# A sparse four-layer graph network on one core: half of a table's copies on VectorE, late variances on ScalarE, sends held back, ring slots freed by whole blocks

## The chip, the cores and the metric

The kernel runs on one NeuronCore of a Trainium2 chip. The core has five engines with instruction queues of their own: TensorE (PE), VectorE (DVE), ScalarE (ACT), GpSimd (POOL) and SyncE (SP). The metric is the device time of one execution in microseconds.

## The reference

A graph of 4096 nodes with 256 features passes through four layers of graph attention. The adjacency matrix `adj` is 4096 x 4096 int32, symmetric, with ones on its diagonal and few others. Every layer normalizes, applies a relu, lets each node attend to its neighbours, and adds the result to `x`:

```python
def _layernorm(x, axis=-1, eps=1e-5):
    m = jnp.mean(x, axis=axis, keepdims=True)
    v = jnp.var(x, axis=axis, keepdims=True)
    return (x - m) / jnp.sqrt(v + eps)

# layer 0: four heads, leaky_relu 0.2, softmax over neighbours, elu
Wh = (h @ W).reshape(n, heads, d)
e = leaky_relu(s_i[:, None, :] + s_j[None, :, :], 0.2)   # s_i, s_j: Wh . a
e = where((adj == 0)[:, :, None], -inf, e)
out = elu(einsum('ijh,jhd->ihd', softmax(e, axis=1), Wh))
# layer 1: one head, slope 0.01, returns h + att @ node, with h = node @ W
# layer 2: four heads, slope 0.2, weights, biases and phis
# layer 3: q, k, v with biases, scores q.k / 8, mask from adj, att @ v
for layer in layers:
    x = x + layer(maximum(_layernorm(x), 0))
```

## The kernel before

The class `Sparse` computes with lists of neighbours and not with the dense matrix. Nodes stand in 32 blocks of 128, sorted by their number of neighbours; `CAPS` gives the largest number in each block, from 23 down to 3. A block's rows lie on the 128 partitions.

**Scan (`scan`, L254).** SP loads `adj` in 128 pieces of 512 KB, ACT turns each into fp8 and sums it (L277, six raw buffers), PE multiplies it by marks (L519, L529), and DVE takes the eight largest of each stretch (L531); from these ACT writes the numbers of the neighbours (L566, L569). Beside that, `tick(k)` (L371) makes the first table: `table(u)` takes a pair of blocks through relu (L342), transposes (L349), ACT's copy from PSUM (L352), two products (L986) and the copies of the products from PSUM to SBUF (L356); SP writes four blocks at a time to the table in DRAM. The scales of a group of four blocks come from `stats` (DVE's sums and ACT's logarithm), `roots` and `scaled`, which `tick` issues at every second pair. `cast(upto)` keeps ACT's casts going between the pairs. Then POOL fetches the first six neighbours of each node (L993, tile `s_g`), one indirect DMA for one neighbour of 128 nodes, and PE sums them.

**Late (`late`, L1056).** The remaining neighbours of the first layer, 19 groups of one or two blocks in the order `LATE`, 93 gathers. `fill(i)` (L1097) first sends out finished rows by `deliver()` (L1086, one indirect DMA of a block's rows of the second table, L1010), then fetches up to four groups ahead into the ring `s_ring`. `settle(i)` (L1195) adds the sums, takes the elu, calls `norms_of` (L636: DVE's BATCH_NORM_STATS2 at L642 and BATCH_NORM_AGGREGATE at L643, ACT's logarithm, exponential and square, three small operations of DVE), then relu, transposes, ACT's copy (L1224), the product with the next weights and the copy of the rows to send (L1233). A block is put on the list `pending` when its rows are made. POOL's order is given by hand: a send comes behind the fetch before it, and the next fetch behind the send.

**Layers 1 to 3 (`layer(l)`, L1263).** For each of the 32 blocks in `ORDER`, `fill` (L1273) fetches the neighbours' rows of the block four places ahead into the ring (`AHEAD`; 18432 floats a partition, which makes 69, 64, 69 and 36 slots in layers 0 to 3), 270 gathers a layer. Then come `scores` (L1359), `weigh` and `settle`. `weigh` multiplies the block's slots by their shares on DVE (L1466, eight slots at once) and lets PE add them up in PSUM (tile `s_acc`): x (L1450), the node's own row `s_me` (L1458), then two slots at a time (L1471). `settle` adds the two halves of the sum on DVE (L1491, or L1487 in layer 3); `normed` and `turned` make the next h, its transposes (L974) and ACT's copy (L976), and `advance` makes the next table's rows. The table's rows go to DRAM on SP, and layer 3's results by POOL (L1010, `out_dram`). The first gather of layer 1 waits for every send of late; the first of layers 2 and 3 wait for the whole table.

The blocks run interleaved: block i is scored and weighed while block i−1 is settled and block i−2 goes through the product. A gather into a slot waits for the product that last read the slot; PE's products each signal for that. All engines run in program order here, so whatever stands behind a waiting instruction on its engine waits too.

## Time and profile before

| | |
|---|---|
| median of four runs | 2037.8 us (2027.78 to 2039.83) |
| profiled execution | 2025.78 us, span 2024.1 us |
| granted TensorE clock, mean | 0.754 |
| busy: PE, DVE, ACT, POOL | 1132.6, 1111.6, 534.9, 1141.2 us |
| POOL's indirect DMAs, gathers into `s_ring` and `s_g` | 900 and 192 |
| sends to the second table | 32 |
| HBM read, written | 273.00 MB, 35.00 MB |

A line of the groups reads: source line, engine, operation, output tile <- input tiles, shapes, number of instructions | busy time, mean time of one in ns | idle time of the engine just before them, and what ended most of it. In a timeline, the start and the duration stand in front of an instruction and the idle time before it and its releaser behind. A line of waits gives the total, the number and the longest wait. Lines are those of the kernel before.

### The profile page before, as it was taken

How to read it: one execution, taken by the hardware profiler on the slowest of the kernel's cores; microseconds unless marked ns; L12 is line 12 of the kernel's file. 1: busy time of each engine (PE TensorE's matmuls, PEld its weight loads, DVE VectorE, ACT ScalarE, POOL GpSimd, SP SyncE). 2: the span in 40 equal slices, each digit the busy share in tenths (PEclk: the TensorE clock that was granted, in tenths of full speed). 3: DMA queues.
4: the chain of work that ended last, by engine and by line, in shares of the span. 5: the costliest groups of instructions: out<-in, count | busy, mean ns of one | idle time of the engine just before them, and what ended most of it. 6: DMA issues, size and time to landing. Idle time of an engine off the chain costs nothing. (4 is left out here: it accounts for less than half of the span.)

```text
span 2024.1 us, 14506 instructions
## 1 busy us (share of the span) xinstructions
PE 1132.6 (56%) x3035; PEld 582.5 (29%) x3035; DVE 1111.6 (55%) x2651; ACT 534.9 (26%) x1754; POOL 1141.2 (56%) x1241
## 2 busy tenths in 40 slices
PE   6678777415673354566773146556669334545545
PEld 4323322113341122333441023223335112222222
DVE  5476777533682233344552125555558466777857
ACT  6854552011252022233341012222335000000000
POOL 1455656776545756666614756565530656766664
PEclk9877777756796676787886667788889566767768
DMA  7999885574422433444412434333321656666663
GB/s 256 339 348 313 305 301 179 183 193 126 131 74 79 118 98 102 110 113 116 115 38 78 109 88 111 97 107 96 99 75 37 197 168 177 202 179 191 176 180 104
DMA packets 125913, 309.12 MB, mean 153 GB/s; under 512 B 35029, under 2 KB 53464, under 8 KB 125817
## 3 DMA queue, kind: packets, MB, share of 16 engines
q0 software_dynamic: 66832, 203.64, 35.5%
q1 hardware_dynamic: 58984, 104.46, 14.7%
q8 instruction: 28, 0.46, 0.1%
q14 instruction: 69, 0.56, 0.1%
HBM read 273.00 MB, written 35.00 MB: 152 GB/s over the span
## 5 line engine op out<-in xcount | busy, mean ns | idle before, releaser
L993 POOL DMA_INDIRECT s_ring<-s_tab,s_near x900 | 853.5, 948 | 581.0 <-issue 255.4
L1471 PE MATMUL s_acc<-s_ring,s_ident 128*128 128x512 f32 (+1 forms) x858 | 422.2, 643 | 32.1 <-issue 19.1
L993 POOL DMA_INDIRECT s_g<-s_tab,s_keep x192 | 183.4, 955 | 178.6 <-DMA s_raw<-in_adj_dram 67.4
L1471 PEld LDWEIGHTS s_acc<-s_ring,s_ident 128*128 128x128 f32 x858 | 183.4, 218 | 249.5 <-issue 213.4
L1466 DVE TENSOR_TENSOR s_ring<-s_ring,s_shares 128x2048 f32<-128x2048 f32 (+1 forms) x153 | 233.0, 1554 | 0.0
L986 PE MATMUL s_ps<-s_we_l,s_ht 128*128 128x264 f32 x256 | 95.3, 518 | 176.7 <-issue 75.8
L1491 DVE TENSOR_REDUCE s_rx<-s_acc 128x256 f32<-128x512 f32 x64 | 44.1, 689 | 253.9 <-remote 180.4
L986 PE MATMUL s_ps_kv<-s_wkv,s_ht 128*128 128x512 f32 x128 | 87.9, 823 | 156.7 <-issue 95.5
L1458 PE MATMUL s_acc<-s_me,s_ident 128*128 128x256 f32 x192 | 74.2, 474 | 174.3 <-DVE s_me L1454 95.8
L519 PE MATMUL s_pt<-s_low,s_mark_True 128*128 128x512 fp8e4 x256 | 97.0, 464 | 72.2 <-ACT s_keep L569 23.7
L277 ACT ACTIVATE s_low<-s_raw 128x1024 fp8e4<-128x1024 int32 x128 | 133.8, 1046 | 12.0 <-DMA s_raw<-in_adj_dram 7.2
L976 ACT COPY s_ht<-s_pht 128x256 f32<-128x256 f32 x64 | 23.8, 372 | 361.5 <-remote 232.1
L986 PEld LDWEIGHTS s_ps<-s_we_l,s_ht 128*128 128x128 f32 x256 | 58.1, 245 | 204.2 <-ACT s_ht L976 80.8
L1418 ACT ACTIVATE s_shares<-s_e 128x40 f32<-128x40 f32 (+7 forms) x64 | 12.6, 197 | 334.1 <-DVE s_e L1415 142.9
L531 DVE MAX8 s_cand<-s_pt 128x8 f32<-128x256 f32 x256 | 93.3, 418 | 13.8 <-PE s_pt L529 13.8
L629 PE MATMUL s_ae<-s_g,s_ident 128*128 128x512 f32 x192 | 95.8, 629 | 2.5 <-DVE s_g L620 2.1
L1458 PEld LDWEIGHTS s_acc<-s_me,s_ident 128*128 128x128 f32 x192 | 41.1, 229 | 191.6 <-DVE s_me L1454 100.1
L1394 DVE TENSOR_TENSOR s_ring<-s_ring,s_shares 128x2048 f32<-128x2048 f32 (+7 forms) x47 | 78.5, 1671 | 17.8 <-DMA s_ring<-s_tab,s_near 17.7
L986 PEld LDWEIGHTS s_ps_kv<-s_wkv,s_ht 128*128 128x128 f32 x128 | 28.5, 247 | 187.5 <-issue 121.7
L1397 DVE TENSOR_REDUCE s_e<-s_ring 128x32 f32<-128x2048 f32 (+7 forms) x47 | 78.9, 1679 | 1.6
L1487 DVE TENSOR_REDUCE s_out<-s_acc 128x256 f32<-128x512 f32 x32 | 22.0, 687 | 90.6 <-remote 67.3
L1010 POOL DMA_INDIRECT s_tab<-s_rx,s_near x32 | 32.8, 1025 | 66.4 <-ACT s_rx L1233 44.9
(284 smaller groups left out, 1797.9 us busy)
## 6 DMA issues: line engine op xcount, KB each, us to landing
s_raw<-in_adj_dram SPq DMA_DIRECT2D x128, 512.0 KB
s_ring<-s_tab,s_near POOLq DMA_INDIRECT x900
s_rx<-s_placed SPq DMA_DIRECT2D x32, 262.0 KB
s_tab<-s_kv SPq DMA_DIRECT2D x32, 256.0 KB
s_tab<-s_rx SPq DMA_DIRECT2D x32, 132.0 KB
s_keep<-in_x_dram SPq DMA_DIRECT2D x8, 512.0 KB
s_vself<-s_tab SPq DMA_DIRECT2D x32, 128.0 KB
s_tab<-s_keep SPq DMA_DIRECT2D x7, 528.0 KB
```

What stands on the lines that cost most here:

```text
L277: nc.scalar.activation(low[r][:, quarter(q)], raw.pop(q), AF.Copy, saturate=False, accum_out=self.sums[:, r, h : h + 1],)
L519: nc.tensor.matmul(pt, lhsT=self.mark[k], rhs=lo[:, k * PAIR + g * IB : k * PAIR + (g + 1) * IB], start=(k == 0), stop=False,)
L531: nc.vector.max(out=cand[:, g * (IB // CH) + k, :], in_=pt[:, ts(k, CH)])
L629: nc.tensor.matmul(acc, lhsT=self.ident, rhs=g[:, :, k, 0:D], start=False, stop=(k == E - 1))
L986: self.nc.tensor.matmul(ps[:, :width], lhsT=ht[:, c, :], rhs=w[:, c, :], start=(c == 0 and bias is None), stop=(c == KC - 1),)
L993: return self.nc.gpsimd.indirect_dma_start(out=out, out_offset=None, in_=table[:, :], in_offset=bass.IndirectOffsetOnAxis(ap=idx, axis=0),)
L1394: nc.vector.tensor_tensor(kq, kq, q.unsqueeze(1).to_broadcast([P, m, D]), ALU.mult)
L1397: nc.vector.tensor_reduce(e[:, k0 : k0 + m, :], kq.rearrange("p k (h d) -> p k h d", h=4), AX.X, ALU.add)
L1458: nc.tensor.matmul(acc[:, 0, :], lhsT=self.ident, rhs=mev, start=False, stop=False)
L1466: nc.vector.tensor_tensor(v, v, p[:, k0 : k0 + m, :].unsqueeze(3).to_broadcast([P, m, H, D // H]), ALU.mult)
L1471: nc.tensor.matmul(acc[:, 0:n, :], lhsT=self.ident, rhs=g[:, k : k + n, v0 : v0 + D], start=False, stop=(k + 2 >= G),)
L1491: nc.vector.tensor_reduce(xt, acc.rearrange("p u d -> p d u"), AX.X, ALU.add)
```

## The change

- In the first table, one of the two copies of a pair (L356) is made by DVE instead of ACT. `tick` issues `roots` and `scaled` at odd places, behind the pairs, and `stats` at even ones; `constants()` is called at place 5 instead of 4, and the casts run one place later (`cast(k - 5)`).
- In late, `settle` takes the sums of x and of its squared deviations by accumulating operands (DVE's sum per block, ACT's square per block) instead of the statistics of `norms_of`.
- `deliver(8)` in late's `fill` holds back the last eight blocks; what is left goes at the end. `known()` is called at group 3 instead of 1. In layer 3 up to three finished blocks are held before one is sent.
- In layers 1 to 3 the node's own row is added last (it was second), the first slot has a product of its own, and then come pairs. The first gather of a block waits for the last product of every old block that its slots overlap (`past`); the other gathers wait for no product. Some dependencies are declared as covered by others (`declare_no_dep`).

```diff
--- before.py
+++ after.py
@@ -352,8 +352,8 @@
             nc.scalar.copy(ht, pt.rearrange("p (k c r) -> p k c r", k=2, c=KC))
             ps = [self.times(ht[:, k], self.we0, W, f"t0_{2 * u + k}") for k in range(2)]
             yield
-            for k in range(2):
-                nc.scalar.copy(self.keep[:, 2 * u + k, D : D + W], ps[k])
+            for k, copy in ((0, nc.scalar.copy), (1, nc.vector.tensor_copy)):
+                copy(self.keep[:, 2 * u + k, D : D + W], ps[k])
             g = u // 2
             m = 2 if g == groups - 1 else 4
             if u % 2 or m == 2:
@@ -376,11 +376,11 @@
                 if u in made:
                     next(made[u])
             g = k // 2 + 1
-            if k % 2 == 0 and g < groups:
+            if k % 2 and g < groups:
                 roots(g)
-                if g + 1 < groups:
-                    stats(g + 1)
                 scaled(g)
+            if k % 2 == 0 and g + 1 < groups:
+                stats(g + 1)
 
         whole = []
         for j in range(nt // 2):
@@ -415,10 +415,10 @@
 
         for k in range(2 * groups + 2):
             tick(k)
-            if k == 4:
+            if k == 5:
                 self.constants()
             if k >= 6:
-                cast(k - 4)
+                cast(k - 5)
             if k - 8 in range(8):
                 mark(k - 8)
         for at in range(8, end + 1):
@@ -1039,6 +1039,7 @@
             self.norms = big.tile([P, 2, nt], F32, name="s_norms")
             self.both = big.tile([P, 2], F32, name="s_both")
             self.has = big.tile([P, nt, CAPS[0]], F32, name="s_has")
+            self.past, self.took_x, self.seen = [], {}, []
             E = mybir.EngineType
             with tc.manual_schedule(engines={E.PE, E.DVE, E.Activation, E.SP}):
                 self.reload()
@@ -1083,8 +1084,8 @@
             self.fetched = f
             return f
 
-        def deliver():
-            while pending:
+        def deliver(held_back=0):
+            while len(pending) > held_back:
                 b = pending.pop(0)
                 s = self.send(self.tab[1], self.own(b), self.listed[b]).ins
                 if self.fetched is not None:
@@ -1096,7 +1097,7 @@
 
         def fill(i):
             nonlocal at
-            deliver()
+            deliver(8)
             while todo and todo[0] <= i + 4:
                 m, K = size(todo[0])
                 s = (at if at + m * K <= slots else 0) if K else 0
@@ -1202,18 +1203,34 @@
             nc.scalar.activation(ex, ex, AF.Copy, bias=-1.0)
             yield
             nc.vector.scalar_tensor_tensor(ex, ex, 0.0, xt, ALU.min, ALU.add)
-            nc.vector.scalar_tensor_tensor(xt, acc, 0.0, ex, ALU.max, ALU.add)
-            norm = self.norms_of(pool, xt if m > 1 else xt[:, 0, :], m, f"0_{i}", self.minus)
-            for _ in range(m if m > 1 else 0):
-                next(norm)
-            next(norm)
+            y = pool.tile([P, 8, 2], F32, name=f"s_y_0_{i}", tag="y0", bufs=3)
+            sum_, minus, q, log, root, less, r, at = (y[:, k, 0:m] for k in range(8))
+            for u in range(m):
+                nc.vector.scalar_tensor_tensor(
+                    xt[:, u, :], acc[:, u, :], 0.0, ex[:, u, :], ALU.max, ALU.add,
+                    accum_out=sum_[:, u : u + 1],
+                )
+            act = nc.scalar.activation
+            act(minus, sum_, AF.Copy, scale=-1.0 / D)
+            junk = pool.tile([P, D], F32, name=f"s_junk_{i}", tag="junk", bufs=1)
+            for u in range(m):
+                act(
+                    junk, xt[:, u, :], AF.Square, bias=minus[:, u : u + 1],
+                    accum_out=q[:, u : u + 1],
+                )
+            act(log, q, AF.Ln, bias=self.eps, scale=1.0 / D)
+            act(less, q, AF.Identity, bias=self.minus, scale=-0.5 / D)
+            act(root, log, AF.Exp, scale=-0.5)
+            act(log, root, AF.Square)
             yield
-            rn = next(norm)
+            nc.vector.tensor_tensor(less, log, less, ALU.mult)
+            nc.vector.scalar_tensor_tensor(r, less, 1.5, root, ALU.add, ALU.mult)
+            nc.vector.tensor_tensor(at, minus, r, ALU.mult)
             h = part(i, D, 2 * D)
             for u in range(m):
                 nc.scalar.activation(
                     h[:, u, :], xt[:, u, :], AF.Relu,
-                    bias=rn[:, m + u : m + u + 1], scale=rn[:, u : u + 1],
+                    bias=at[:, u : u + 1], scale=r[:, u : u + 1],
                 )
             pt = self.pp.tile([P, IB], F32, tag="ps", name=f"s_pht_0_{i}")
             for u in range(m):
@@ -1244,7 +1261,7 @@
 
         for i in range(len(LATE) + 3):
             fill(i)
-            if i == 1:
+            if i == 3:
                 self.known()
             if i == 5:
                 self.share_place()
@@ -1269,6 +1286,7 @@
         ring = self.ring[:, : slots * wide].rearrange("p (k w) -> p k w", w=wide)
         todo, held, at = list(ORDER), {}, 0
         made = []
+        past = self.past
 
         def fill(i):
             nonlocal at
@@ -1287,9 +1305,27 @@
                 if l == 3:
                     vs[j] = self.pool.tile([P, D], F32, name=f"s_vself_{j}", tag="vself", bufs=5)
                     nc.sync.dma_start(out=vs[j], in_=self.tab[3][ts(j, P), D:])
+                ends = [
+                    e for a, b, e in past if a < (s + room) * wide and s * wide < b
+                ]
+                past[:] = [
+                    (a, b, e) for a, b, e in past if not (a < (s + room) * wide and s * wide < b)
+                ]
                 for k in range(K):
                     at_k = self.near[:, j, k : k + 1]
                     g = self.fetch(ring[:, s + k, :], self.tab[l], at_k).ins
+                    if k == 0:
+                        for _, last in ends:
+                            self.tc.add_manual_dep(
+                                g, last.name,
+                                mybir.DependencyInfo(
+                                    mybir.DependencyClass.Sync, mybir.DependencyReason.DATA
+                                ),
+                                reason="the block's slots are free",
+                            )
+                    for some, _ in ends:
+                        for m in some:
+                            self.tc.declare_no_dep(g, m, reason="its block's last is waited for")
                     for told in self.told:
                         self.tc.add_manual_dep(
                             g, told.name,
@@ -1328,7 +1364,7 @@
         def third(d):
             if d in rows:
                 next(rows.pop(d), None)
-            while made and (len(made) > 1 or todo == []):
+            while made and (len(made) > 3 or todo == []):
                 self.send(*made.pop(0))
 
         S, N = 1, 2
@@ -1343,7 +1379,8 @@
             third(e)
             product(d)
             sums[b] = self.weigh(l, b, vs.pop(b) if l == 3 else self.rows[b][:, 0:D], g, p)
-            del held[b]
+            start, end = held.pop(b)
+            past.append((start * wide, end * wide, self.read))
             settle(c)
         z, y, x, w = ORDER[-1:-5:-1]
 
@@ -1371,7 +1408,7 @@
                 nc.scalar.activation(e[:, :G, 0], g[:, :G, D], AF.Identity, bias=src)
                 nc.scalar.activation(e[:, K, :], mine[:, D : D + H], AF.Identity, bias=src)
             else:
-                nc.vector.tensor_tensor(e[:, K, :], mine[:, D : D + H], src, ALU.add)
+                first = nc.vector.tensor_tensor(e[:, K, :], mine[:, D : D + H], src, ALU.add)
                 nc.vector.tensor_tensor(
                     e[:, :G, :], g[:, :G, D : D + H],
                     src.unsqueeze(1).to_broadcast([P, G, H]), ALU.add,
@@ -1383,7 +1420,9 @@
             if more:
                 self.more_scores(l, mine, g[:, KEPT, :], e)
             slope = 0.01 if l == 1 else 0.2
-            nc.vector.scalar_tensor_tensor(ek, ek, slope, ek, ALU.mult, ALU.max)
+            steep = nc.vector.scalar_tensor_tensor(ek, ek, slope, ek, ALU.mult, ALU.max)
+            if l == 2:
+                self.tc.declare_no_dep(steep.ins, first.ins, reason="another sum comes after it")
         else:
             q = self.shares[:, IB - D :]
             nc.scalar.copy(q, mine[:, 0:D])
@@ -1426,7 +1465,9 @@
         nc.vector.tensor_scalar(
             eq[:, :K, :], g[:, :K, W : WL - 1], self.own_f[:, b : b + 1], None, ALU.is_equal
         )
-        nc.vector.tensor_reduce(self.has[:, b, :K], eq[:, :K, :], AX.X, ALU.max)
+        self.seen.append(
+            nc.vector.tensor_reduce(self.has[:, b, :K], eq[:, :K, :], AX.X, ALU.max).ins
+        )
 
     def weigh(self, l, b, me, g, made):
 
@@ -1447,18 +1488,22 @@
         self.turns += 1
         v0 = 0 if l < 3 else D
         acc = self.pacc.tile([P, 2, D], F32, tag="acc", name=f"s_acc_{l}_{b}")
-        nc.tensor.matmul(
+        self.took_x[b] = nc.tensor.matmul(
             acc[:, 1, :], lhsT=self.ident, rhs=self.x[b], start=True, stop=False
         )
+        some = []
         mev = pool.tile([P, D], F32, name=f"s_me_{l}_{b}", tag="me", bufs=3)
-        nc.vector.tensor_tensor(
+        own = nc.vector.tensor_tensor(
             mev.rearrange("p (h d) -> p h d", h=H), me.rearrange("p (h d) -> p h d", h=H),
             p[:, K, :].unsqueeze(2).to_broadcast([P, H, D // H]), ALU.mult,
         )
-        nc.tensor.matmul(acc[:, 0, :], lhsT=self.ident, rhs=mev, start=False, stop=False)
         if more:
             rows = self.more_rows(l, p, g[:, KEPT, :])
-            nc.tensor.matmul(acc[:, 0, :], lhsT=self.to_row, rhs=rows, start=False, stop=False)
+            some.append(
+                nc.tensor.matmul(
+                    acc[:, 0, :], lhsT=self.to_row, rhs=rows, start=False, stop=False
+                ).ins
+            )
         step = 2 if b in ORDER[-2:] else AT_ONCE
         for k0 in range(0, G, step):
             m = min(step, G - k0)
@@ -1466,12 +1511,21 @@
             nc.vector.tensor_tensor(
                 v, v, p[:, k0 : k0 + m, :].unsqueeze(3).to_broadcast([P, m, H, D // H]), ALU.mult
             )
-            for k in range(k0, k0 + m, 2):
-                n = min(2, G - k)
-                nc.tensor.matmul(
-                    acc[:, 0:n, :], lhsT=self.ident, rhs=g[:, k : k + n, v0 : v0 + D],
-                    start=False, stop=(k + 2 >= G),
-                )
+            k = k0
+            while k < k0 + m:
+                n = min(2, k0 + m - k) if some else 1
+                some.append(
+                    nc.tensor.matmul(
+                        acc[:, 0:n, :], lhsT=self.ident, rhs=g[:, k : k + n, v0 : v0 + D],
+                        start=False, stop=False,
+                    ).ins
+                )
+                k += n
+        last = nc.tensor.matmul(
+            acc[:, 0, :], lhsT=self.ident, rhs=mev, start=False, stop=True
+        ).ins
+        self.tc.declare_no_dep(last, own.ins, reason="the slots' products come after it")
+        self.read = (some, last)
         return acc
 
     def settle(self, l, b, acc, made):
@@ -1488,7 +1542,10 @@
             made.append((self.out, self.own(b), y))
             yield None
             return
-        nc.vector.tensor_reduce(xt, acc.rearrange("p u d -> p d u"), AX.X, ALU.add)
+        s = nc.vector.tensor_reduce(xt, acc.rearrange("p u d -> p d u"), AX.X, ALU.add)
+        self.tc.declare_no_dep(
+            s.ins, self.took_x.pop(b).ins, reason="the sum's last product comes after it"
+        )
         yield from self.normed(pool, xt, f"{l + 1}_{b}")
 
     def advance(self, l, b, ht, made):
@@ -1530,9 +1587,11 @@
     def symmetric(self):
 
         nc, ok = self.nc, self.ok[:, 4:5]
-        nc.vector.scalar_tensor_tensor(
+        all_of = nc.vector.scalar_tensor_tensor(
             self.has, self.away[:, :, : CAPS[0]], 1.0 / FAR, self.has, ALU.mult, ALU.max
         )
+        for i in self.seen[:-1]:
+            self.tc.declare_no_dep(all_of.ins, i, reason="the last of them is waited for")
         nc.vector.tensor_reduce(self.both[:, 0:1], self.has, AX.XY, ALU.min)
         nc.vector.tensor_reduce(ok, self.both, AX.X, ALU.min)
         nc.vector.tensor_scalar(ok, ok, 0.5, None, ALU.is_ge)
```

## Prediction

> **What bounds the kernel now.** I read the page's groups first, then the waits of POOL, then the timeline at one place, then windows. No engine is busy for more than 57% of the span (PE 1132.6 us, DVE 1111.6, POOL 1141.2 of 2024.1), so the end is set by turns between engines. Groups of the page (busy time, mean ns, idle time before them, what ended it):
>
> ```profile
> L993 POOL DMA_INDIRECT s_ring<-s_tab,s_near x900 | 853.5, 948 | 581.0 <-issue 255.4
> L1491 DVE TENSOR_REDUCE s_rx<-s_acc 128x256 f32<-128x512 f32 x64 | 44.1, 689 | 253.9 <-remote 180.4
> L976 ACT COPY s_ht<-s_pht 128x256 f32<-128x256 f32 x64 | 23.8, 372 | 361.5 <-remote 232.1
> L1487 DVE TENSOR_REDUCE s_out<-s_acc 128x256 f32<-128x512 f32 x32 | 22.0, 687 | 90.6 <-remote 67.3
> ```
>
> A gather costs POOL 0.95 us and 0.30 us to the next ("issue", 255.4 us over about 800 of them), so 1.25 us. The three readers of PE's results in PSUM wait 254 + 362 + 91 us for something that the profile calls "remote". The timeline shows what it is:
>
> ```profile
> 663.02 8.96 PE L1471 MATMUL s_acc<-s_ring,s_ident 128*128 128x512 f32 x16 [0.98 <-issue]
> 701.82 0.69 DVE L1491 TENSOR_REDUCE s_rx<-s_acc 128x256 f32<-128x512 f32 x1 [33.45 <-issue]
> 705.79 0.69 PE L974 MATMUL s_pht<-s_ident,s_h 128*128 128x128 f32 x2 [31.23 <-issue]
> 727.78 0.95 POOL L993 DMA_INDIRECT s_ring<-s_tab,s_near  x1 [0.30 <-issue]
> 729.83 0.37 ACT L976 COPY s_ht<-s_pht 128x256 f32<-128x256 f32 x1 [22.79 <-remote]
> 741.20 0.94 POOL L993 DMA_INDIRECT s_ring<-s_tab,s_near  x1 [12.47 <-ACT s_rx L1507]
> ```
>
> PE's sums of block 0 are recorded done at 671.98, and DVE starts to add them at 701.82. PE's two transposes are done at 706.48, ACT copies them at 729.83: 1.1 us after POOL's last gather of an unbroken row ended (728.73). Meanwhile nearly everything but POOL stands still; columns of the windows: length, then busy (instructions) of PE, PEld, DVE, ACT, POOL, clock, DMA share, GB/s:
>
> ```profile
> 670.00:700.00 30.00, 4.56 (x14) 2.28 (x12) 0.00 (x0) 0.00 (x0) 22.68 (x24) 0.63 0.44 118
> 1498.50:1574.00 75.50, 66.20 (x198) 36.48 (x198) 58.21 (x144) 35.95 (x140) 0.04 (x1) 0.96 0.11 40
> ```
>
> The first stretch has 24 gathers and nothing on DVE and ACT. The second is layer 2's tail without gathers: there the same work goes at full pace. My reading: while POOL issues gathers without a break, PE's completions reach the other engines late, and they come through when POOL pauses. A layer thus alternates between a gathering POOL and computing engines, instead of doing both. That it depends on how many completions PE signals is my assumption; no row shows it alone. POOL's own waits (total, times, longest) say what the pauses are:
>
> ```profile
> POOL s_ring L993 <- PE s_acc L1471: 85.8, 37, 9.1
> POOL s_ring L993 <- DMA s_vself<-s_tab: 75.8, 1, 75.8
> POOL s_ring L993 <- DMA s_tab<-s_rx: 56.6, 1, 56.6
> POOL s_tab L1010 <- ACT s_rx L1233: 44.9, 10, 10.1
> ```
>
> Stages by POOL's first DMA: late 413.2, layer 1 632.8, layer 2 1080.2, layer 3 1574.4, last send ends 2020.6.
>
> **The change, part by part.** The sum is made on the profiled execution, 2025.8 us (span 2024.1 and 1.7 around it); the median of the four runs is 2037.8, 0.6% above, and I scale at the end.
>
> **First table.** 16 of 32 copies of L356 (0.38 us each) leave ACT, 6.1 us, from an engine that is busy 9.94 of 10 us in 40–50; DVE, busy 4.77 there, takes them. Turning the roots behind the pairs, and the cast by one place, moves work in the same queues and with each cast the issue of a raw load on SP: ACT's casts (1.05 us each) come one tick later, which could cost up to three of them, 3.1 us. Then DMA at 300–350 GB/s sets the scan. Between −6.1 and +3.1; I take −3, the ACT time less one such cast.
>
> **Late variances.** DVE loses 32 x (0.414 + 0.182) = 19.1 us of statistics (L642, L643) and gains 13 further starts where a two-block sum of L1205 is cut in two, some 0.2 us each: net −17. ACT gains 32 squares with an accumulator (0.42 + 0.19) and 19 small operations of 0.23: +24, on 69.3 us in a stage of 219.6. DVE is the busier there (52.1 of 60 us in 550–610), ACT has 30 us free in the same window. Between −17 and +7 (ACT's gain less DVE's loss, if the chain of a group runs through both); nearest to −12.
>
> **Sends held back.** POOL waits 44.9 us for L1233 and 15.3 for L1224 ahead of sends: these go for the first 66 gathers, which now run in one row from 413 to 496 (66 x 1.25). Behind the waiting sends stood the gathers. But the pause at 470.5–481.6 is also what let PE's completions through, in a burst at 478.5; now they wait for about 497. The work behind it moves by up to 20 us. The 60 us that POOL no longer waits can't be had whole: the last groups are bound by DVE, and 22 sends now stand at the end (x 1.3 = 29 us). So between −31 and +20; nearest is the row of the burst, +20, of which I take off the 15 us for L1224: +5. known() at i == 3 moves a few DVE operations behind the first groups: nothing, hidden by DVE's wait for the first gathers there.
>
> **Blockwise freeing.** Removed: the signal of most products. In the built programs PE signals 1184 times before and 651 after on the sparse path; in layers 1 and 2 about 9.5 times a block becomes 4 (last product, transposes, scores' two tables), in layer 3 6.5 becomes 1. POOL's separate waits on PE fall from 440 to 121; a satisfied one cost nothing in the trace (gap of 0.30 us with and without). Added: one matmul of 256 columns (0.43 us) in blocks of an even number of slots, on a PE that idles half of the layer: nothing, covered by DVE's next product of 1.55 us. Also added: the first gather of a block waits for the last product of every old block that it overlaps. Behind this gather stand all later gathers on POOL, and behind these, the scores of four blocks on. In layer 2 POOL already stalls 22 times for L1471 (67.0 us); each would end later by the rest of a block, at most four products x 0.86 = 3.4 us. By the ring's layout (64, 69 and 36 slots) a gathered block overlaps two old ones 5, 5 and 4 times. Over 5 (layer 2's borders) to 22 stalls that is +17 to +75, if POOL were the bound throughout.
> Layer bounds: POOL alone needs 270 x 1.25 = 337.5 us a layer. Layer 1 gathers in 390.8 us (53 over) and then waits 56.6; layer 2 in 418.1 (81 over) and waits 75.8; layer 3 takes 446, with 32 sends x 1.3 = 42 and a tail of 28 in it, so 39 over.
> With half the completions I take that a quarter to a third of the excess goes: layer 1, 53 x 0.28 = −15 (ends −53 − 7 of tail, and +5); layer 2, 81 x 0.25 = −20 (ends −81, and +75 by the stalls above); layer 3, with one completion of PE in six left and 91 us of DVE waiting for just these, 28 of the 39 (ends −39 − 11 of POOL's waits for L1487 ahead of sends, and +11 if keeping sends until four are made moves these waits into the gathers). What is late next is then DVE's products (304.6 us busy in layer 3) and POOL's row.
>
> The Trainium skill, VectorE: DVE Perf Modes, section "The DRAIN you can't avoid", speaks against the largest part: eight copies took 13.88 us with a semaphore after each and with one after the last, "the semaphore costs nothing extra here". That is VectorE on its own; the 22.8 us at ACT's copy of L976 is a cross-engine wait that it does not cover. If it held for PE, an estimate by that page would put the blockwise part at zero and the sum at −10.
>
> Sum: table −3, late −12 + 5 = −7, layers −15 − 20 − 28 = −63: −73. 2025.8 − 73 = 1953; on the median, 2037.8 x 1953/2025.8 = 1965.
>
> **Rivals.**
> *Slower: waiting for whole blocks starves POOL.* One mechanism: the first gather at the border of two blocks waits for the newer one's last product. For it: layer 2's 22 stalls, up to 9.1 us, and the 14 borders. Against it: in layers 1 and 3 POOL hardly waits for L1471 (1.8 and 17.0 us). Without any gain from earlier completions it decides from three such stalls on (10/3.4), with all of mine from 22 (73/3.4). With 5 to 22 of them and no gain, +17 to +75, less 10 for table and late: 2045 to 2103 on the median.
> *No change: the number of completions does not matter.* If each pause of POOL lets all through and no unbroken row lets any, the alternation keeps its period. For it: the flushes in the scan stand 19 us apart, just where POOL pauses. Then table and late remain, −10: 2028, from 2018 to 2043.
> *Larger gain: compute keeps up with gathering.* If PE's completions come promptly, each layer nears POOL's own 337.5 us plus a tail of four blocks at 7.8 us (31, by 1498–1574): layer 1 −79, layer 2 −125, layer 3 −45, late −7, table −3, −259 at the end of the range; half of it is 1908. Against it: layers 1 and 2 still signal four times a block.
>
> **How the numbers follow.** Forecast 1965, 0.50; larger gain 0.15; no change 0.15; slower 0.20. The forecast's own range, by half of the distance to each term's ends, is 1905 to 2015. Less than 0.5% (10 us) from 2037.8 is about what a measurement cannot tell from no change. Faster by more takes the forecast nearly whole, the larger gain, and about a third of "no change": 0.69; within, 0.10; slower, 0.21. The range leaves out a tenth below and less above: 1880, inside the larger gain, to 2080, which is some 60% of the slower rival's span.
>
> **What will show it.** ACT's 232.1 us of "remote" at L976 and DVE's 180.4 at L1491 fall by a third or more, L1487's 67.3 to under 20. POOL's waits for s_acc stay under 110 us. Layer 3 takes under 425 us from its first gather to the last send, layer 1 under 435. In the late stage POOL has no wait for L1233 before 496 and DVE's first sums come near 497. I am wrong if ACT's and DVE's waits stay while PE signals half as often, or if POOL's waits at blocks' first gathers grow by more than they fall.

## The result and the profile after

The changed kernel takes 2029.92 us (median of 44 runs, 2017.67 to 2047.95), the kernel before 2030.56 us in 70 runs. The ratio is 1.0001, 95% interval 0.9986 to 1.0016: no change, where the forecast was 1965 us. The profiled executions took 2022.11 us (span 2020.4) and 2025.78 us (span 2024.1).

The groups of the changed kernel that answer to those shown of before; L1545, L1541 and L1518 are the lines that were L1491, L1487 and L1471:

```profile
L993 POOL DMA_INDIRECT s_ring<-s_tab,s_near x900 | 853.7, 949 | 548.1 <-issue 298.8
L1545 DVE TENSOR_REDUCE s_rx<-s_acc 128x256 f32<-128x512 f32 x64 | 44.0, 687 | 224.6 <-remote 182.7
L976 ACT COPY s_ht<-s_pht 128x256 f32<-128x256 f32 x64 | 23.7, 370 | 278.3 <-remote 219.1
L1541 DVE TENSOR_REDUCE s_out<-s_acc 128x256 f32<-128x512 f32 x32 | 22.0, 687 | 78.0 <-remote 40.4 <-PE s_acc L1524 18.6 <-issue 14.4
```

The waits called remote have hardly moved at the first two: 182.7 us beside 180.4 at DVE's sum, 219.1 beside 232.1 at ACT's copy. At layer 3's sum (L1541) they fell from 67.3 to 40.4. The timeline at the same place, block 0 of layer 1:

```profile
704.69 8.94 PE L1518 MATMUL s_acc<-s_ring,s_ident 128*128 128x512 f32 x16 [0.98 <-issue]
743.99 0.69 DVE L1545 TENSOR_REDUCE s_rx<-s_acc 128x256 f32<-128x512 f32 x1 [32.74 <-issue]
747.97 0.69 PE L974 MATMUL s_pht<-s_ident,s_h 128*128 128x128 f32 x2 [31.33 <-issue]
772.03 0.37 ACT L976 COPY s_ht<-s_pht 128x256 f32<-128x256 f32 x1 [22.83 <-remote]
```

PE's sum is recorded done at 714.05 and DVE starts 29.9 us later; before, it was 29.8 us. Of the block's products only the last signals now, and the wait is the same. Windows of the changed kernel:

```profile
714.05:743.99 29.94, 2.59 (x11) 1.55 (x9) 0.00 (x0) 0.00 (x0) 22.63 (x25) 0.59 0.44 118
500.00:530.00 30.00, 0.00 (x0) 0.00 (x0) 0.00 (x0) 0.00 (x0) 13.90 (x15) 0.50 0.38 108
```

The second stretch is new: 30 us in late in which PE, DVE and ACT do nothing at all. It ends with ACT's first sum behind POOL's row of gathers, which in the kernel before came 50 us earlier. The line of before, then that of the changed kernel:

```profile
480.23 0.38 ACT L1201 ACTIVATE s_ex<-s_acc 128x256 f32<-128x256 f32 x1 [11.09 <-PE s_acc L1190]
530.17 0.38 ACT L1202 ACTIVATE s_ex<-s_acc 128x256 f32<-128x256 f32 x1 [64.82 <-remote]
```

Where the time went, by POOL's first DMA of each stage, in us (the end is the last send's):

| | until late | late | layer 1 | layer 2 | layer 3 | end |
|---|---|---|---|---|---|---|
| before | 413.2 | 219.6 | 447.4 | 494.2 | 446.2 | 2020.6 |
| changed | 417.2 | 257.8 | 443.5 | 461.6 | 436.2 | 2016.4 |
| difference | +4 | +38 | −4 | −33 | −10 | −4 |

So the tie is made of a gain of 47 us in the layers and a loss of 42 us ahead of them. The sends show where late lost it. POOL's waits in the changed kernel (total, times, longest), L1250 and L1241 being what were L1233 and L1224:

```profile
POOL s_tab L1010 <- ACT s_rx L1250: 50.5, 11, 7.2
POOL s_tab L1010 <- ACT s_ht L1241: 38.2, 6, 10.8
```

They have grown from 44.9 + 15.3 to 88.7 us, though the sends stand eight blocks further back. The gathers gained nothing either: late's last one ends at 579.4 us, before at 581.3. But the work that should have run beside them is still to do. The rest of late behind the last gather, before and then changed:

```profile
581.00:632.80 51.80, 32.18 (x109) 19.34 (x108) 35.06 (x122) 24.68 (x86) 14.79 (x16) 0.91 0.13 44
579.40:675.00 95.60, 67.14 (x204) 39.49 (x204) 58.58 (x214) 55.73 (x200) 22.52 (x23) 0.87 0.10 36
```

PE has 67.1 us of products left there instead of 32.2, and the rest of late is 44 us longer: that is where the loss appears.

### The profile page after: what moved, and what is told of

The parts are those of the page before. It is cut to its first block, busy times and chain, and to the rows that moved or that the text cites. A ratio compares the mean times of both kernels' runs of the same rounds, so it can differ in the third digit from the quotient of the medians.

```text
span 2020.4 us, 14691 instructions
## 1 busy us (share of the span) xinstructions
PE 1116.1 (55%) x3179; PEld 609.1 (30%) x3179; DVE 1096.4 (54%) x2648; ACT 554.0 (27%) x1821; POOL 1141.0 (56%) x1241
## 4 chain that ended last, share of the span: by engine, by line
DVE 29%; issue 23%; another core or an unknown queue 15%; PE 11%; ACT 8%; POOL 8%; DMA 4%; DVEq 0%; SPq 0%; ACTq 0%; POOLq 0%
DVE s_ring L1511 6%; POOL s_ring L993 5%; PE s_acc L1518 4%; DVE s_cand L531 3%; DVE s_ring L1433 2%; PE s_ps_kv L986 2%; DMA s_ring<-s_tab,s_near 2%; DVE s_g L620 2%; DMA s_raw<-in_adj_dram 1%; POOL s_placed L720 1%; DVE s_e L1436 1%; DVE s_top L543 1%; DVE s_rx L1545 1%; DVE s_cand L545 1%
## 5 line engine op out<-in xcount | busy, mean ns | idle before, releaser
L1518 PE MATMUL s_acc<-s_ring,s_ident 128*128 128x512 f32 (+1 forms) x1002 | 432.1, 586 | 203.7 <-DVE s_ring L1511 112.7
L1518 PEld LDWEIGHTS s_acc<-s_ring,s_ident 128*128 128x128 f32 x1002 | 219.6, 223 | 392.5 <-issue 252.4
L1545 DVE TENSOR_REDUCE s_rx<-s_acc 128x256 f32<-128x512 f32 x64 | 44.0, 687 | 224.6 <-remote 182.7
L986 PE MATMUL s_ps_kv<-s_wkv,s_ht 128*128 128x512 f32 x128 | 82.5, 778 | 129.3 <-ACT s_ht L976 77.1
L976 ACT COPY s_ht<-s_pht 128x256 f32<-128x256 f32 x64 | 23.7, 370 | 278.3 <-remote 219.1
L956 ACT ACTIVATE s_y<-s_mv,s_eps 128x1 f32<-128x1 f32 x64 | 18.9, 295 | 203.3 <-DVE s_mv L953 44.3
L519 PEld LDWEIGHTS <-s_mark_True 128*128 128x128 bf16 x256 | 24.0, 106 | 142.4 <-issue 100.1
L1491 PE MATMUL s_acc<-s_rx,s_ident 128*128 128x256 f32 x192 | 66.0, 429 | 0.0
```

The lines of the kernel that those rows point to most:

```text
L519: nc.tensor.matmul(pt, lhsT=self.mark[k], rhs=lo[:, k * PAIR + g * IB : k * PAIR + (g + 1) * IB], start=(k == 0), stop=False,)
L986: self.nc.tensor.matmul(ps[:, :width], lhsT=ht[:, c, :], rhs=w[:, c, :], start=(c == 0 and bias is None), stop=(c == KC - 1),)
L1491: self.took_x[b] = nc.tensor.matmul(acc[:, 1, :], lhsT=self.ident, rhs=self.x[b], start=True, stop=False)
L1518: nc.tensor.matmul(acc[:, 0:n, :], lhsT=self.ident, rhs=g[:, k : k + n, v0 : v0 + D], start=False, stop=False,).ins
L1545: s = nc.vector.tensor_reduce(xt, acc.rearrange("p u d -> p d u"), AX.X, ALU.add)
```

## The experiments

Each kernel was timed on one chip beside the kernel before; ratios are to that, with the 95% interval in brackets. Stage times are from one profiled execution each. In nine executions of kernels that have the same code in a layer, layer 1 took 442.2 to 444.2 us, but layer 2 459.0 to 479.9 and layer 3 434.4 to 445.6, so a stage time of one execution says little about 10 us in layer 3 or 20 in layer 2.

### Each part alone

The sends alone, on the kernel before:

```diff
-        def deliver():
-            while pending:
+        def deliver(held_back=0):
+            while len(pending) > held_back:
...
-            deliver()
+            deliver(8)
```

> The kernel before with one edit: late's sends held back by eight blocks. Theory A (holding back costs what the blocks of slots gain: after's late stage took 257.8 us against 219.6, its layers 1 to 3 46 us less): 38 us slower than before, ratio 1.015 to 1.022, with ACT's first sum after POOL's unbroken row waiting past 520 us. Rival B (the late stage grew by ACT's variances, not by the sends): ratio 0.99 to 1.005, late under 225 us. Rival C (the stages only shift by chance): within 0.5%.

Measured: 2059.0 us, ratio 1.0098 [1.0063, 1.0132]; late takes 252.2 us. ACT's first sum behind POOL's row, in the timeline of this kernel:

```profile
525.84 0.38 ACT L1201 ACTIVATE s_ex<-s_acc 128x256 f32<-128x256 f32 x1 [55.09 <-remote]
```

Theory A has the sign and the place, but the ratio lies below its range: the price by the medians is 27 us, less than the 33 of the stage.

The changed kernel without it:

```diff
-            deliver(8)
+            deliver(0)
```

> The changed kernel with one edit: late's sends are not held back (all other parts as changed). Theory A: 38 us of late come back, ratio to before 0.977 to 0.985; POOL's pause before its first send lies near 480 us, PE's results flow from there. Rival B: late stays above 245 us, ratio 0.995 to 1.005.

Measured: 1993.52 us, ratio 0.9825 [0.9788, 0.9862], late 224.9 us. As theory A has it: 36 us come back with this one edit.

The layers' part alone (late and the first table as before):

> The kernel before with the layers' part alone: own row last, first slot alone, gathers released by whole blocks (and layer 3's sends held by three); first table and late as before. Theory A: layers 1 to 3 take 40 to 50 us less than before (443 + 462 + 436 against 447 + 494 + 446), ratio 0.975 to 0.983. Rival C (the layers' gain is a consequence of another phase at their start): the gain is under 15 us, ratio over 0.992.

Measured: 1997.91 us, ratio 0.9844 [0.9808, 0.988]: 34 us less by the medians, a little less than theory A has it. Its layers take 442.2, 461.4 and 439.2 us, about as in the changed kernel, though layer 1 starts here at 638.9 us and there at 675.0. The gain does not hang on where the layers start.

The changed kernel with a wait for each slot:

```diff
-                    if k == 0:
-                        for _, last in ends:
-                            self.tc.add_manual_dep(g, last.name, ...)
-                    for some, _ in ends:
-                        for m in some:
-                            self.tc.declare_no_dep(g, m, ...)
```

> The changed kernel, but each gather waits for the product that last read its own slot, so that PE signals per product as it did before (533 more signals); own row last, first slot alone and all other parts as changed. If the number of PE's signals or the waiting for whole blocks is what gained in the layers: 35 to 50 us slower than the changed kernel, ratio to before 1.015 to 1.025. If the order of the products and the dropped dependencies made the gain, or it is chance: within 0.5% of the changed kernel.

Measured: 2093.6 us, ratio 1.0284 [1.0242, 1.0325], more than expected. Layers 1 to 3 take 465.3, 493.5 and 452.4 us. The freeing by blocks, with the signals that it saves, is the gain; the new order of the products without it is 18 us slower in layer 1 than the old order was (one execution each).

Late wholly as before, with the changed layers and first table (statistics on DVE, `deliver(0)`, `known()` at group 1):

> The changed kernel with late wholly as before (sends at once, statistics on DVE, known() at group 1): the first table's and the layers' parts are left. Against the kernel with sends at once but the variances on ACT (ratio 0.9825) it prices the variances, against the layers' part alone (0.9844) the first table. If the variances save the 12 us forecast: ratio 0.985 to 0.991. If ACT's added work eats DVE's gain: 0.976 to 0.985. First table as forecast (-3 us): 0.1 to 0.2% under the layers' part alone.

Measured: 1989.15 us, ratio 0.981 [0.9757, 0.9863], the lowest of all here, though the intervals of its neighbours overlap with it. Neither the variances on ACT (0.9825 with them) nor the first table (0.9844 without it) shows a gain beside it.

### What holds PE's results back

Both kernels of this part are the changed one with other fills of layer 2's slots:

```diff
-                    g = self.fetch(ring[:, s + k, :], self.tab[l], at_k).ins
+                    if l == 2:
+                        for _ in range(3):
+                            g = nc.gpsimd.memset(ring[:, s + k, :], 0.0).ins
+                    else:
+                        g = self.fetch(ring[:, s + k, :], self.tab[l], at_k).ins
```

> The changed kernel, but in layer 2 POOL fills each slot by three memsets of 128x264 instead of a gather (the neighbours' rows of layer 2 are left out, so its sums hold zeros). POOL stays about as busy, no software DMA goes. If POOL's DMA holds PE's results back: in layer 2, ACT's and DVE's waits called remote at the copy of the transposes and at the sum of the halves fall from 83 + 80 us to under 15, and the layer takes 250 to 330 us instead of 461. If a busy POOL as such does it: these waits stay above 60 us and the layer above 420.

```diff
-                    g = self.fetch(ring[:, s + k, :], self.tab[l], at_k).ins
+                    if l == 2:
+                        g = nc.sync.dma_start(
+                            out=ring[:, s + k, :], in_=self.tab[l][ts((j + k) % nt, P), :]
+                        ).ins
+                    else:
+                        g = self.fetch(ring[:, s + k, :], self.tab[l], at_k).ins
```

> The changed kernel, but in layer 2 SP brings 128 rows in sequence into each slot by a plain DMA instead of POOL's gather (layer 2 gets other rows than its neighbours'). The same bytes go to the same places, POOL stays still. If POOL's DMA issue or its queue holds PE's results: the remote waits of layer 2 fall under 15 us, the layer takes 250 to 340 us. If the bytes landing in SBUF do it: the waits stay above 60 us, the layer above 400.

Measured: 1851.44 and 1855.24 us in one run each. From the last gather of layer 1 to the first of layer 3 it takes 330.3 and 329.4 us instead of 509.4. Groups of the first one (POOL's between 1060 and 1400 us, the others between 1100 and 1396), then of the second one the window of layer 2, its waits and DVE's sum between 1100 and 1400 us:

```profile
L1318 POOL MEMSET s_ring<- 128x264 f32 x807 | 241.7, 318 | 46.9 <-PE s_acc L1528 10.3 <-ACT s_y L962 5.6
L976 ACT COPY s_ht<-s_pht 128x256 f32<-128x256 f32 x34 | 12.2, 360 | 4.7 <-PE s_pht L974 4.6
L1549 DVE TENSOR_REDUCE s_rx<-s_acc 128x256 f32<-128x512 f32 x34 | 23.3, 685 | 7.0 <-PE s_acc L1528 7.0
```

```profile
1119.40:1401.00 281.60, 249.62 (x790) 146.17 (x790) 235.68 (x574) 122.83 (x483) 0.95 (x1) 0.96 0.55 160
```

```profile
ACT s_ht L976 <- PE s_pht L974: 68.0, 32, 3.0
```

```profile
L1550 DVE TENSOR_REDUCE s_rx<-s_acc 128x256 f32<-128x512 f32 x34 | 23.4, 687 | 11.7 <-PE s_acc L1529 11.6
```

With POOL busy for 241.7 us by memsets, ACT waits 4.7 us at its copy and DVE 7.0 at its sum. With the rows brought by SP at 160 GB/s, there is no remote wait either; ACT's 68.0 us are 32 short waits for PE itself, which is busy 250 of 282 us. So neither a busy POOL nor that traffic holds PE's results; POOL's own DMAs do. Whether it is their issue, their queue or their scattered rows, these two kernels don't tell apart.

Not all of the 179 us by which this stretch gets shorter are the price of the holding, since POOL's own time for 270 gathers goes too. In the runs below in which results are not held, the same stretch with its gathers takes 389.3 us (the kernel with late's slots freed by groups).

### Why the sends matter

A pause of POOL put into late's row of gathers, in the changed kernel:

```diff
+                        row[0] += 1
+                        if row[0] == 44:
...
+                            for _ in range(16):
+                                m_ = nc.gpsimd.memset(still, 0.0).ins
...
```

> The changed kernel with one edit: in late, after 44 gathers in a row, POOL writes zeros into a scratch tile 16 times (128x768, about 0.7 us each by the 0.83 us of L484's 128x896, so some 11 us), then goes on. Theory: PE's results come through when POOL issues no DMA for a few us, so the pause gives back what held back sends cost, though it costs POOL 11 us: ACT's first sum after the row comes before 490 us instead of 530, late takes 222 to 245 us instead of 257.8, ratio to before 0.983 to 0.995. Rival: what matters is that the sends themselves come early: late stays at 255 us or grows to 270, ratio 0.998 to 1.008.

Measured: 2028.09 us, ratio 1.0012 [0.998, 1.0044], late 254.3 us. Timelines of POOL, ACT and PE in this kernel:

```profile
474.00 12.69 POOL L1118 MEMSET s_still<- 128x768 f32 x16
486.84 0.95 POOL L993 DMA_INDIRECT s_ring<-s_tab,s_near  x1 [0.16 <-issue]
```

```profile
482.46 0.38 ACT L1211 ACTIVATE s_ex<-s_acc 128x256 f32<-128x256 f32 x1 [13.46 <-PE s_acc L1200]
531.00 0.38 ACT L1211 ACTIVATE s_ex<-s_acc 128x256 f32<-128x256 f32 x1 [27.12 <-remote]
542.21 0.59 ACT L1250 COPY s_ht<-s_pht 128x512 f32<-128x512 f32 x1 [10.21 <-issue]
```

```profile
542.85 2.57 PE L986 MATMUL s_ps<-s_we_l,s_ht 128*128 128x264 f32 x5 [38.34 <-issue]
```

The pause did what was said: ACT's sum comes at 482.46, 8.5 us after POOL's last DMA, instead of 530.17. The time was not given back. POOL goes on at 486.84, with no send that has to wait until 552, and in this second row PE stands still for 38.34 us. The rival has the number. In the kernel before, sends wait for their rows again and again, at 471.5 us for 10.1 us, then for 4.8, 2.8 and 5.2 us by 552; that these waits work like the pause put in here is argued, not shown.

Two rows show that "they come through when POOL pauses" is too simple. In the second row ACT's next sum comes at 531.00, some 27 us behind its products, and its copy at 542.21, some 38 us behind the transposes, while POOL's row runs on without a break until 552.35. And in the changed kernel POOL stands still from 511.93 on for 5.1, 3.3 and 2.6 us between single gathers, and nothing reaches ACT before 530.17. POOL's DMAs delay PE's results; what sets the length of the delay was not found.

With half of the blocks held back (the layers and the first table as changed, late otherwise as before):

> The kernel with late as before and the changed layers and first table (ratio 0.981), with sends held back by four blocks instead of none (eight took 35 us). If the cost comes with each send that no longer stops POOL's row of gathers: about half, 12 to 24 us, late 235 to 247 us, ratio 0.987 to 0.994. If only the very first row matters (PE's results held until it ends): the first send at 485 to 490, and late 223 to 232, ratio 0.981 to 0.986.

> The kernel with late as before and the changed layers and first table, with sends held back by four blocks. Where PE's results are held: if the cost comes with each send that no longer stops POOL's row of gathers, late takes 235 to 247 us, ratio 0.987 to 0.994; if only the first row matters, late 223 to 232, ratio 0.981 to 0.986. Where they are not held: ratio 1.002 to 1.005 again.

The first time it ran where PE's results are not held: 1.0037 [1.0022, 1.0051], of which more below. Measured where they are held: 2010.77 us, ratio 0.9894 [0.9833, 0.9956], late 240.0 us. With 0, 4 and 8 blocks held back late takes 223.4, 240.0 and 257.8 us (the last with the variances on ACT), and ACT's first sum behind the row starts at 481.53, 506.14 and 530.17. By the stage the cost grows with the number of sends held back, as the first expectation has it; the ratio's interval reaches into the second as well.

### Signals or waits

The last product alone signals, and POOL waits once a block: the change does both. To tell them apart, SP waits for each product in layers 1 and 2 and then writes 4 bytes, so that PE signals 398 times more, while POOL waits as changed (late as before):

```diff
         self.read = (some, last)
+        if l < 3:
+            for m_ in some:
+                told = nc.sync.dma_start(
+                    out=self.signs[n_ : n_ + 1, :], in_=self.ident[0:1, 0:1]
+                ).ins
+                self.tc.add_manual_dep(told, m_.name, ...)
```

> The kernel with late as before and the changed layers and first table (ratio 0.981), and in layers 1 and 2 each product of the slots signals again: an idle SP waits for each and then writes 4 bytes to a scratch place. POOL's gathers wait by whole blocks as in the changed kernel. If the number of PE's signals is what cost the time: layer 2's gathers take 410 to 420 us instead of 392, the pauses behind layers 1 and 2 go back to 55 to 60 and 75 us from 48 and 70, ratio 0.992 to 1.002. If the waiting by whole blocks is what gains: layer 2's gathers within 5 us of 392, ratio 0.979 to 0.985.

> The kernel with late as before and the changed layers and first table, where SP waits for each product of the slots in layers 1 and 2, so that PE signals 398 times more. Where PE's results are held: if the number of signals costs the time, layer 2's gathers take 410 to 420 us instead of 392 and the ratio is 0.992 to 1.002; if the waiting by whole blocks is what gains, they stay within 5 us of 392, ratio 0.979 to 0.985. Where they are not held: ratio 1.002 to 1.004 again.

> The kernel with late as before and the changed layers and first table, where SP waits for each product of the slots in layers 1 and 2, so that PE signals 398 times more, in five rounds. The four kernels with the layers' part and sends at once stand at 0.981 to 0.984 where PE's results are held, this one stood at 0.988 [0.983, 0.994]. If the number of signals takes part in the gain: 0.986 to 0.992, the interval above 0.984. If it was chance: 0.981 to 0.985. Where they are not held: 1.002 to 1.004.

Measured where results are held (the second): 2010.99 us, ratio 0.9884 [0.9827, 0.994], layer 2 483.2 us. Where they are not (the first and third): 1.0028 [1.0016, 1.0039] and 1.003 [1.002, 1.004], beside 1.0032 without the signals, so that there a signal costs nothing that can be measured.

The other way round, late's slots freed by whole groups while PE signals as often:

> The kernel with late as before and the changed layers and first table (ratio 0.981), and in late too the first gather of a group waits for the last product of every old group that it overlaps, the other gathers for none: POOL's waits on PE there fall from 47 to 6. PE's products of late still signal each, 66 times. If the gain in the layers comes from POOL's waiting once a block: late gets 5 to 20 us shorter than its 223 us, ratio 0.971 to 0.979. If it comes from the number of PE's signals: late within 4 us of 223, ratio 0.979 to 0.983.

> The kernel with late as before and the changed layers and first table, with late's slots freed by whole groups too: POOL's waits on PE there fall from 47 to 6, PE signals as often. Where PE's results are held: since the signals restored in the layers took back some 20 of the 32 us of layer 2, the rest is the waiting by whole blocks; in late, with a third as many gathers that wait, that would be 2 to 6 us: late 217 to 222 instead of 223, ratio 0.976 to 0.983. If waiting by whole groups makes longer rows and more holding: late 226 to 235, ratio 0.983 to 0.989. Where they are not held: 1.002 to 1.005 again.

Measured: 0.9836 [0.9771, 0.9901] with late 221.7 us where results are held, 1.0032 [1.002, 1.0045] where they are not. Late did not get shorter by more than executions differ.

What follows is limited. The kernel with the signals back lies between the two expectations, and its interval overlaps that of the one without (0.9757 to 0.9863). Its layer 2 took 483.2 us, but that of the kernel with late's groups, which has no extra signals in the layers, took 479.6. Its gathers of layer 2 took 410.6 us, as expected if signals cost the time, beside 400.3 there. Clearest is layer 1: 448.3 us, outside the 442.2 to 444.2 of nine executions without the extra signals and level with the kernel before (447.4). But the execution profiled is the slowest of five, 13 us above their median. Both parts point to the signals rather than the waits; neither settles it.

### Layer 3's sends

```diff
-            while made and (len(made) > 3 or todo == []):
+            while made and (len(made) > 1 or todo == []):
```

> The kernel with late as before and the changed layers and first table, with layer 3's results sent as before (two made, one sent) and not held until four are made. Where PE's results are held: if each wait of POOL for a result is a pause that lets PE's results through, as in late, layer 3 gets shorter, 425 to 434 us instead of 435 to 445, ratio 0.975 to 0.981; if these waits only cost POOL's time (10.9 us before), 5 to 11 us longer, ratio 0.983 to 0.987. Where they are not held: layer 3 within 3 us of 405, ratio 1.001 to 1.006.

The kernel it is set against, late's slots freed by groups, ran on the same chip and differs from this one by that freeing too, with late at 219.8 and 221.7 us. Measured: 2003.34 us, ratio 0.9881 [0.9848, 0.9914], against 1991.55 us, and layer 3 446.7 against 434.4 us. POOL's waits ahead of layer 3's sends, of this kernel and then of the one with late as before, which holds up to three:

```profile
POOL out_dram L1010 <- DVE s_out L1525: 20.6, 3, 8.8
```

```profile
POOL out_dram L1010 <- DVE s_out L1525: 2.3, 1, 2.3
```

Here holding back seems to help, by some 12 us, the opposite of late, as the second expectation has it. It is not shown: the two intervals overlap, and kernels that hold back took up to 445.6 us in layer 3.

### The same kernels where results are not held

In two sets of runs the kernel before takes 1676.93 us (14 runs, 1674.23 to 1680.68) and 1677.45 us (17 runs), instead of 2030. The record numbers the chips: 7, 10 and 14 where it takes some 2030 us, 9 and 10 where it takes 1677. So number 10 stands on both sides, some eight minutes apart, and whether the same number means the same piece is not on record. That it is the chip which makes the difference is therefore not shown. The groups there, of the kernel with late's slots freed by groups:

```profile
L993 POOL DMA_INDIRECT s_ring<-s_tab,s_near x900 | 855.6, 951 | 328.5 <-issue 291.5 <-DMA s_ring<-s_tab,s_near 12.2 <-PE s_acc L1531 2.7
L1552 DVE TENSOR_REDUCE s_rx<-s_acc 128x256 f32<-128x512 f32 x64 | 43.8, 685 | 13.2 <-PE s_acc L1531 13.2
L976 ACT COPY s_ht<-s_pht 128x256 f32<-128x256 f32 x64 | 23.4, 365 | 27.2 <-PE s_pht L974 27.1
```

A gather, a sum and a copy take what they take elsewhere; the waits called remote are gone but for 3.1 us in the scan. Even PE's own products run closer together. Both of the next views are of late, beside an unbroken row of POOL's DMAs: first two products of the changed kernel where results are held, then 16 of the kernel above where they are not.

```profile
471.24 0.59 PE L1191 MATMUL s_acc<-s_ring,s_ident 128*128 128x256 f32 x1 [2.23 <-issue]
474.03 0.59 PE L1191 MATMUL s_acc<-s_ring,s_ident 128*128 128x256 f32 x1 [2.20 <-issue]
```

```profile
423.79 4.23 PE L1210 MATMUL s_acc<-s_ring,s_ident 128*128 128x256 f32 x16
```

One product in 2.8 us stands beside 16 in 4.2, so PE's next products seem to be delayed as well as its results. Late takes 177.4 us, the layers 361.4, 365.1 and 406.3. The ratio of four kernels with the changed layers and first table is 1.003 to 1.007 there: the gain of these parts turns into a loss of 5 us or more. The variances, beside the same kernel without them:

> The changed kernel with sends at once and late's slots freed by whole groups (the variances stay on ACT, known() at group 3). Beside the same with statistics on DVE it prices the variances again: within 0.4% of it if ACT's added 24 us and DVE's 17 us cancel; 0.6% under it if DVE's time alone counts.

Measured: 1.0066 [1.0049, 1.0083] against 1.0032, late 182.3 against 177.4 us. On ACT they cost 5 us (`known()` two groups later included). The changed kernel itself was run once more:

> The changed kernel once more beside the kernel before. On a chip where the kernel before takes some 2030 us (PE's results are held while POOL gathers): ratio 0.997 to 1.003, late 250 to 260 us, layer 2 460 to 465. On a chip where it takes some 1677 us (they are not held): nothing of what the blocks of slots gained is left and late loses by the held sends and ACT's variances, 5 to 12 us slower, ratio 1.003 to 1.009; late 184 to 190 us beside 177 with sends at once.

Results were held in these runs: 2033.4 us, ratio 1.0003 [0.9972, 1.0034], late 255.2 us, layer 2 464.8 us. They repeat the result; the change as a whole was not measured where results are not held.

## Why the prediction was wrong

**What bounds the kernel.** That POOL's row of gathers holds back PE's results was right, and is shown by the two kernels without layer 2's gathers. (The 254 + 362 + 91 us are all the idle time of the three readers; 480 of these 707 us are called remote.) Wrong in part is "they come through when POOL pauses": they also came 27 to 38 us late inside an unbroken row, and pauses of 5 us and less let nothing through to ACT.

**Sends held back: the step that failed most.** The sum had +5, with +20 as the upper end; it is +27 on the kernel before and +36 in the changed one. "These go for the first 66 gathers" was right: the first send now stands behind 66 gathers. But ACT's first sum came at 530 where "about 497" was named, and the work behind it moved by 50 us, not by up to 20. What failed is the step from POOL's waits to time: "the 60 us that POOL no longer waits can't be had whole" counts these waits as a loss of which part comes back, and takes off 15 us for L1224. None came back; they grew to 88.7 us, and the gathers ended no earlier (579.4 us beside 581.3). The work that had run in and behind POOL's waits came after the last gather instead. The prediction applied its own reading to one pause only, that at 470.5–481.6, and not to the later ones.

**Blockwise freeing: right in sign, wrong in the way.** Forecast −15, −20 and −28; the profiled executions give −4, −33 and −10, the part alone −34 by the medians instead of −63. The step "with half the completions I take that a quarter to a third of the excess goes" failed: PE's results came no earlier to ACT's copy and DVE's sum in layers 1 and 2. This is the sign that the prediction itself gave for being wrong: their waits stayed (219.1 and 182.7 us) with 651 signals of PE instead of 1184. What fell is the time of POOL's rows: layer 2's gathers took 392.0 us instead of 418.3, layer 3's 405.4 instead of 417.9, while layer 1's went from 390.9 to 395.7. The feared stalls by whole blocks did not come. In layer 3, "with one completion of PE in six left", L1487's remote wait fell from 67.3 to 40.4 us, not to under 20, and the layer gained 10 us by the executions profiled: the two kernels with the old layer 3 took 446.2 and 440.4 us, nine with the new one 434.4 to 445.6. How much of it belongs to the held sends, which had no gain in the sum, and how much to the signals stays open: with the sends as before layer 3 took 446.7 us, with the sends held but a signal for each slot 452.4.

**Late variances.** −12 forecast; no gain that can be measured where results are held, +5 where they are not. The saving of DVE's 17 us was counted as if late were bound by DVE. Where results are held, late is bound by the delay behind POOL's rows; that ACT's longer chain for a group makes the 5 us is argued, not shown.

**First table.** −3 forecast, +4 in the table of stages, and late started at 412.5 to 416.2 us in three kernels with the old table and at 414.4 to 422.6 in twelve with the new one. No gain is visible; the casts' later place, the upper end of that term, may have taken it.

**The range and the rivals.** The forecast's own range, 1905 to 2015, does not follow from its rule: half of the distance to each term's ends gives 1878 to 2062. In the larger gain, the −45 for layer 3 does not follow from the bound that gives −79 and −125; that bound gives −78, or −36 with the 42 us of sends. "No change" had the number, 2028, but by luck: the freeing does move the time, and the sends move it back. Its cause, that the number of completions does not matter, holds for block 0 of layer 1, whose sum waits as long with one signal, and is not shown for a whole layer.

## What to carry to other kernels

Ask of an idle engine what its pause lets through before you remove the wait that makes it. Here POOL's waits in late were worth more than the gathers that could have run in them, while those ahead of layer 3's sends seem not to have been; the timeline behind the pause tells, not the length of the wait. When a change has several parts, a forecast near zero can be a large gain and a large loss: the four kernels with the layers' part and sends at once stand at 0.981 to 0.984.

## What was not expected of the hardware

POOL's indirect DMAs delay PE's results on their way to the other engines. A POOL that is busy with memsets does not (ACT's wait 4.7 us), nor do as many bytes brought by SP (no remote wait). After POOL's last DMA before the pause put in, it took 8.5 us until the first held sum was used; in an unbroken row results came 27 and 38 us late.

It is not always so. In most of the runs the kernel before takes some 2030 us, in two sets of them 1677 us with the same program, 17% less, and there the waits are gone from the trace. The layers' part and the first table, worth 1.9% where results are held, are in kernels that lose 0.3% where they are not. What sets the two apart was not found: nothing in the program does, and one chip number of the record stands on both sides.
